# q and softmax weights read from PSUM in a gathered graph attention, with the last block as its own chunk

## The chip, the cores and the metric

The kernel runs on one core of one Trainium2 chip. The metric is the device time of one execution in microseconds; before the change it is 3077.46 us, the median of three runs (3075.20 to 3083.46). The profile is of one more execution, which took 2989.22 us, with a span of 2987.4 us from the first to the last instruction.

A core has a TensorE (PE, with its weight loads listed apart as PEld), a VectorE (DVE), a ScalarE (ACT) and a GpSimd (POOL), which run their instructions in order and wait for each other by semaphores. Transfers are carried out by 16 DMA engines. SBUF is the working memory, PSUM the memory that PE writes its products to[...].

## The reference

Four graph layers follow each other on 3327 nodes of 256 features. The adjacency matrix is sparse (each entry set with probability 0.0048, about 16 neighbours a node). Layer 0 is a simpler attention; layers 1 to 3 are transformer layers whose attention is masked by the adjacency:

```python
qkv = layer_norm(x, g1, be1) @ w_qkv
q, k, v = ...                                   # [n, 8 heads, 32]
scores = jnp.einsum('nhd,mhd->hnm', q, k) * SCALE
scores = jnp.where(mask, scores, -jnp.inf)      # mask: adj != 0
attn = jax.nn.softmax(scores, axis=-1)
out = jnp.einsum('hnm,mhd->nhd', attn, v).reshape(n, DIM)
x = x + out @ w_proj + b_proj
h2 = layer_norm(x, g2, be2)
ff = jax.nn.gelu(h2 @ w1 + b1) @ w2 + b2        # 256 -> 1024 -> 256
return x + ff
```

## The kernel before

A first part builds each node's list of neighbours, sorts the nodes by degree into 26 blocks of 128 nodes, and computes layer 0. What follows concerns the second part, layers 1 to 3. Block b has CAPS[b] neighbour slots per node (40 for block 0, then 24 down to 10). For each slot, GpSimd gathers the K and V rows (2 KB) of 128 neighbours with one indirect DMA; four slots make a group, and a ring of ten groups holds the gathered rows. Blocks are worked in the order 25, 1, 24, 2, ..., 13, 0.

```python
CAPS = [40, 24, 22, 21, 20, 20, 19, 19, 18, 18, 17, 17, 17,
        16, 16, 15, 15, 15, 14, 14, 13, 13, 12, 12, 11, 10]
GS = 4; NBUF = 10; CB = 4

def issue(self):                                   # one group of gathers
    ...
    for s in range(n):
        nc.gpsimd.indirect_dma_start(              # L1214
            out=t[:, s, :], out_offset=None, in_=kv[L],
            in_offset=bass.IndirectOffsetOnAxis(ap=t2[:, b, k:k + 1].bitcast(U32), axis=0))

def scores(self, b, s0):
    ...
    k = t[:, :n, :D]                               # K product, in place: L1232
    nc.vector.tensor_mul(k, k, t2[:, b, None, D:2 * D].to_broadcast([P, n, D]))
    nc.vector.tensor_reduce(self.sc[b][:, s0:s0 + n, :],              # L1233
                            k.rearrange("p s (h d) -> p s h d", d=HD), AX.X, ALU.add)

def softmax(self, b):                              # the max on DVE (L1244), exp on ACT (L1247)
    ...
def weights(self, b):                              # sums, reciprocal, and sc = sc / sum (L1255)
    ...
def values(self, b, s0):
    ...                                            # V product: L1269
    nc.vector.tensor_mul(vw..., v, self.sc[b][:, s0:s0 + n, :, None].to_broadcast(...))
    for s in range(0, n, 2):                       # PE adds the slots up, with an identity: L1274
        nc.tensor.matmul(self.po[b][:, :m], ident, vw[:, s * D:s * D + m], ...)
    self.issue()                                   # the group's buffer is free again
    if s0 + GS >= S:
        self.short += self.block(b)
```

When a block's values are summed, six short steps project it: copy po (ACT), transpose (PE), copy (ACT), project (PE), nothing, add to x (DVE, L1314). Four blocks make a chunk; once the last of them is projected, the chunk's long steps are queued: norm, transposes, and a feed-forward network on up to 512 columns (up L1352, gelu L1358, down L1367, all with features on partitions), a transpose back (L1373, L1381), an add (L1385), and then the next layer's norm and q, k, v (L1396), stored to DRAM for the next layer's gathers. In layer 3 the rows are scattered to the output instead (L1409). Both queues are taken from between groups:

```python
def some(self):
    for _ in range(2 if len(self.short) > 6 else 1):
        if self.short:
            self.short.pop(0)()
    self.credit = min(self.credit + self.rate, 8.0)
    while self.long and self.credit > 0:
        cost, step = self.long.pop(0)
        self.credit -= cost
        step()

def run(self):
    ...
    for k, b in enumerate(ORDER):
        ...
        for g in slots[b]:
            self.scores(*g)
            ...                                    # one or two values() of earlier blocks
            self.some()
        self.softmax(b)
        ...
    while todo:
        value()
        self.some()
    self.rate = 4.0
    while self.short or self.long:
        self.some()
```

The eight PSUM banks are 2 for po, 2 for the feed-forward sums, 1 for the projection, 3 for everything else. With 26 blocks and chunks of four, the last chunk has two blocks, 13 and 0. The next layer's first gather can start only when all rows of K and V are stored.

Of the kernel before, what the change touches and what calls it, by code (L numbers as in the profile page):

```python
# [17 lines left out]
P = 128  # L18
N = 3327
D = 256  # L20
# [503 lines left out]
def sparse_path(ctx, tc, ins, out, dram, flag):  # L524
# [614 lines left out]
    ps_y = ctx.enter_context(tc.tile_pool(name="b_ps_y", bufs=2, space=PSUM))  # L1139
    ps_r = ctx.enter_context(tc.tile_pool(name="b_ps_r", bufs=1, space=PSUM))  # L1140
    ps_b = ctx.enter_context(tc.tile_pool(name="b_ps_b", bufs=3, space=PSUM))

# [8 lines left out]

    bp3 = big.tile([96, D], BF, name="bp3")
    nc.vector.memset(bp3, 0.0)

    def bank(name):
        return ps_b.tile([P, 512], FP, tag="b", name=name)

    def load_rest(L):
        w = gains(L, ("g2", "be2", "b1", "b2"), wts, bank, "b")
        for name, c, n in (("w_proj", 2, D), ("w1", 2, FF), ("w2", 8, D)):  # L1160
            w[name] = wts.tile([P, c, n], FP, tag=name, name=f"s_{name}_{L}")
            nc.sync.dma_start(w[name], get(L, name).rearrange("(c p) n -> p c n", p=P))
        room = work.tile([P, 2 * D], FP, tag="kvr", name=f"s_row_{L}")
        row, part3 = room[:96, :D], room[:96, D:D + D // 2].bitcast(BF)
        nc.vector.memset(row, 0.0)
        for p in (0, 32, 64):
            nc.sync.dma_start(row[p:p + 1, :], get(L, "b_proj")[None, :])
        for p in (0, 32, 64):
            nc.vector.tensor_copy(part3, row)
            nc.vector.tensor_copy(bp3[p:p + 1, :], part3[p:p + 1, :])  # L1170
            if p < 64:
                nc.vector.tensor_sub(row, row, part3)
        return w
# [7 lines left out]
    ORDER = [b for k in range(NB // 2) for b in (NB - 1 - k, k + 1)][:NB - 1] + [0]  # L1181
    CHUNK = {}
    for k, b in enumerate(ORDER):
        first = k // CB * CB
        CHUNK[b] = ORDER[first:first + CB]
    slots = {b: [(b, s) for s in range(0, CAPS[b], GS)] for b in ORDER}

    class Layer:
        def __init__(self, L, w, nxt):
            self.L, self.w, self.nxt = L, w, nxt  # L1190
            self.groups = [g for b in ORDER for g in slots[b]]
            self.issued = 0
            self.tiles, self.sc, self.po = {}, {}, {}
            self.rows = 0

            self.short, self.long = [], []
            self.rate = self.credit = 0.0
# [20 lines left out]


        def scores(self, b, s0):  # L1220

            L, S = self.L, CAPS[b]
            n = min(GS, S - s0)
            t = self.tiles[b, s0]
            if s0 == 0:
                self.sc[b] = work.tile([P, LMAX, HEADS], FP, tag="sc", bufs=3, name=f"sc_{L}_{b}")
                if L == 1:
                    nc.vector.tensor_scalar(pad[b],
                                            t2[:, b, 2 * D:2 * D + S].bitcast(I32),
                                            0.0, FAR, ALU.is_equal, ALU.mult)  # L1230
            k = t[:, :n, :D]
            nc.vector.tensor_mul(k, k, t2[:, b, None, D:2 * D].to_broadcast([P, n, D]))  # L1232
            nc.vector.tensor_reduce(self.sc[b][:, s0:s0 + n, :],  # L1233
                                    k.rearrange("p s (h d) -> p s h d", d=HD), AX.X, ALU.add)
            if L == 1:
                nc.scalar.copy(t2[:, b, 2 * D + s0:2 * D + s0 + n].bitcast(I32), t[:, :n, 2 * D])
# [12 lines left out]
        def weights(self, b):  # L1249
            L, S = self.L, CAPS[b]  # L1250
            sc = self.sc[b][:, :S, :]
            den = small.tile([P, HEADS], FP, tag="den", name=f"den_{L}_{b}")
            nc.vector.tensor_reduce(den, sc.rearrange("p s h -> p h s"), AX.X, ALU.add)
            nc.vector.reciprocal(den, den)
            nc.vector.tensor_mul(sc, sc, den[:, None, :].to_broadcast([P, S, HEADS]))  # L1255
            nc.vector.tensor_max(least, least, den)

        def values(self, b, s0):
# [4 lines left out]
            if s0 == 0:  # L1263
# [6 lines left out]
                vw[:, :n * D].rearrange("p (s h d) -> p s h d", h=HEADS, d=HD), v,  # L1270
                self.sc[b][:, s0:s0 + n, :, None].to_broadcast([P, n, HEADS, HD]))
            for s in range(0, n, 2):
# [9 lines left out]
        def block(self, b):  # L1282
# [7 lines left out]
            def copy():  # L1290
                c["o"] = work.tile([P, 2 * D], FP, tag="o", name=f"o_{L}_{b}")
                nc.scalar.copy(c["o"], self.po.pop(b))  # L1292

            def turn():
                pt = c["pt"] = bank(f"pto_{L}_{b}")
                for k in range(2):
# [5 lines left out]
            def copy_T():  # L1302
                c["oT"] = work.tile([P, 2 * P], FP, tag="oT", name=f"oT_{L}_{b}")
                nc.scalar.copy(c["oT"], c["pt"][:, :2 * P])

            def project():
                ps = c["ps"] = ps_r.tile([P, 512], FP, tag="r", name=f"ppr_{L}_{b}")
                nc.tensor.matmul(ps[:, :D], ones_bf[:96, :], bp3, start=True, stop=False)
                for k in range(2):
                    nc.tensor.matmul(ps[:, :D], c["oT"][:, k * P:(k + 1) * P], w["w_proj"][:, k, :],  # L1310
                                     start=False, stop=(k == 1))

            def add():
                nc.vector.tensor_add(x, x, c["ps"][:, :D])  # L1314
                n2.stats(chunk.index(b), x)
                if b == chunk[-1]:
                    self.long += self.chunk(chunk, n2)
                    at = ORDER.index(b) + 1
                    turns = sum(len(slots[i]) for i in ORDER[at:at + CB])
                    self.rate = sum(cost for cost, _ in self.long) / max(turns - 2, 1)  # L1320

            return [copy, turn, copy_T, project, lambda: None, add]

        def chunk(self, blocks, n2):
# [10 lines left out]
            def turns(key, tag):  # L1335
                def turn(j):
                    if j == 0:
                        c[tag] = [bank(f"p{tag}_{L}_{b0}_{k}") for k in range(2)]
                    c[key].turn(j, x[j], work, c[tag])
# [21 lines left out]
            def down(f):  # L1361
                if f == 0:
                    c["py"] = [ps_y.tile([P, 512], FP, tag="y", name=f"py_{L}_{b0}_{k}")
                               for k in range(2)]
                g = c.pop(("gT", f))
                for e in range(2):
                    nc.tensor.matmul(c["py"][e][:, :n], w["w2"][:, f, e * P:(e + 1) * P],  # L1367
                                     g[:, :n], start=(f == 0), stop=(f == FF // P - 1))

# [6 lines left out]
            def back(j0):  # L1376
                pb = c["pd", j0] = bank(f"pd_{L}_{b0}_{j0}")
                for j in js[j0:j0 + 2]:
# [12 lines left out]
            def qkv(j):  # L1391
                b = blocks[j]
                pk, pq = c["pk", j], c["pq", j] = bank(f"pk_{L}_{b}"), bank(f"pq_{L}_{b}")
                for ps, c0, c1 in ((pk, D, 3 * D), (pq, 0, D)):
# [26 lines left out]
            F = FF // P  # L1421
            for f in range(F + 3):
                fs = []
                if 0 <= f - 2 < F:
                    fs.append(lambda f=f: gelu(f - 2))
                if 0 <= f - 3 < F:
                    steps.append(at(2 * k, *fs, lambda f=f: down(f - 3)))
                    fs = []
                if f < F or fs:
                    steps.append(at(2 * k, *fs, *([lambda f=f: up(f)] if f < F else [])))  # L1430
            steps += [at(1.5, shift), at(1.5, lambda: back(0))]
            if len(blocks) > 2:
# [15 lines left out]
        def some(self):  # L1448

            for _ in range(2 if len(self.short) > 6 else 1):  # L1450
                if self.short:
                    self.short.pop(0)()
            self.credit = min(self.credit + self.rate, 8.0)
            while self.long and self.credit > 0:
                cost, step = self.long.pop(0)
                self.credit -= cost
                step()

        def run(self):
            for _ in range(NBUF):  # L1460
                self.issue()

            todo, wait = [], {}
# [6 lines left out]
            for k, b in enumerate(ORDER):  # L1470
                while k > 2 and todo and todo[0][0] == ORDER[k - 3]:
                    value()
                for g in slots[b]:
                    self.scores(*g)
                    for i in wait:
                        wait[i] += 1
                    for _ in range(2 if len(todo) > NBUF // 2 else 1):
                        if todo and wait[todo[0][0]] > 1:
                            value()
                    self.some()  # L1480
                self.softmax(b)
                todo += slots[b]
# [52 lines left out]
```

## Time and profile before

| | |
|---|---|
| time, median of 3 | 3077.46 us |
| span of the profiled run | 2987.4 us, mean granted TensorE clock 0.81 |
| busy | PE 68%, DVE 65%, POOL 54%, ACT 25% |
| gathers of K and V (L1214) | 1344, 1132 ns each in the mean |
| K products (L1232), reductions (L1233), V products (L1269) | 363 of each, 416.0, 414.0 and 409.1 us |
| moved | 453.66 MB, 152 GB/s in the mean |

A group row of the profile names the line, the engine, the operation, what it writes and reads, how often, then its busy time, the mean duration of one, and the idle time of its engine before it with what ended it. POOL is busy only while it executes a gather's instruction; the transfer follows on the DMA engines. A window's row gives each engine's busy time and, in brackets, its instructions. Matmuls in fp32 appear as two records each.

### The profile page before, as it was taken

What the parts mean: (1) busy time and instruction counts of PE and PEld (TensorE: products, weight loads), DVE (VectorE), ACT (ScalarE), POOL (GpSimd) and SP (SyncE); (2) the same over time, 40 slices, a digit from 0 to 9 for tenths busy, and PEclk for the clock granted to TensorE, in tenths of its full rate; (3) what the DMA queues carried; (4) which work ended last, traced back from release to release, by engine and by line L of the source; (5) the groups of instructions that cost most, each with busy time, mean ns of one, the idle gap of its engine ahead of it and who ended that gap; (6) DMA issues with size and microseconds to landing.
All of it is one profiled execution on the core that took longest, in us unless ns stands there. A gap on an engine that the chain in (4) does not pass through costs nothing. (4 is left out here: it accounts for less than half of the span.)

```text
span 2987.4 us, 22161 instructions
## 1 busy us (share of the span) xinstructions
PE 2042.1 (68%) x6718; PEld 1113.3 (37%) x6718; DVE 1941.2 (65%) x3998; ACT 754.3 (25%) x1231; POOL 1615.1 (54%) x1461
## 2 busy tenths in 40 slices
PE   4566666514678878787267878787844668668757
PEld 4444444302334444344123444344322334323324
DVE  2977777556777777762477877687336766667652
ACT  2444344100223232232002222232210122222211
POOL 3000000047777777740777777777037777777750
PEclk9677676656898989898578989888966888889878
DMA  4323231147776776661666666666146656556650
GB/s 173 138 101 112 105 121 52 32 160 193 195 201 184 199 198 194 191 136 46 185 182 180 187 182 176 187 180 186 40 122 187 181 160 175 164 166 181 171 141 12
DMA packets 144459, 453.66 MB, mean 152 GB/s; under 512 B 29512, under 2 KB 40138, under 8 KB 141003
## 3 DMA queue, kind: packets, MB, share of 16 engines
q0 software_dynamic: 113056, 370.26, 44.9%
q1 hardware_dynamic: 9816, 53.89, 5.1%
q10 hardware_dynamic: 21458, 28.02, 2.6%
q8 instruction: 54, 0.88, 0.1%
q14 instruction: 75, 0.61, 0.1%
HBM read 420.63 MB, written 31.42 MB: 151 GB/s over the span
## 5 line engine op out<-in xcount | busy, mean ns | idle before, releaser
L1214 POOL DMA_INDIRECT kv<-kv,t x1344 | 1521.7, 1132 | 658.3 <-issue 349.7
L1274 PE MATMUL po<-vw,s_ident 128*128 128x512 f32 (+1 forms) x1380 | 751.6, 681 | 490.2 <-DVE vw L1269 490.0
L1232 DVE TENSOR_TENSOR kv<-kv,t 128x1024 f32<-128x1024 f32 (+3 forms) x363 | 416.0, 1146 | 463.6 <-DMA kv<-kv,t 444.5
L1274 PEld LDWEIGHTS po<-vw,s_ident 128*128 128x128 f32 x1380 | 286.4, 218 | 855.9 <-DVE vw L1269 538.8
L1269 DVE TENSOR_TENSOR vw<-kv,sc 128x1024 f32<-128x1024 f32 (+3 forms) x363 | 409.1, 1139 | 37.2 <-PE po L1274 36.1
L1233 DVE TENSOR_REDUCE sc<-kv 128x32 f32<-128x1024 f32 (+3 forms) x363 | 414.0, 1141 | 12.5
L1352 PE MATMUL pu<-fT,s_w 128*128 128x512 f32 (+1 forms) x672 | 301.5, 582 | 1.3 <-ACT fT L596 1.3
L1367 PE MATMUL py<-gT,s_w 128*128 128x512 f32 (+1 forms) x672 | 291.8, 563 | 0.0
L702 POOL MEMSET s_abf<- 128x1 bf16 x26 | 2.6, 103 | 436.9 <-PE s_ptb L714 251.5
L1352 PEld LDWEIGHTS pu<-fT,s_w 128*128 128x128 f32 x672 | 133.0, 202 | 129.4 <-issue 113.2
L1358 ACT ACTIVATE gT<-pu,pvb 128x512 f32<-128x512 f32 (+1 forms) x168 | 110.1, 657 | 278.1 <-PE pu L1352 277.9
L1367 PEld LDWEIGHTS py<-gT,s_w 128*128 128x128 f32 x672 | 127.7, 191 | 128.6 <-issue 123.9
L714 PE MATMUL s_ptb<-s_ident_bf,s_abf 128*128 128x128 bf16 x676 | 76.5, 292 | 114.6 <-ACT s_aT L715 83.4
L1292 ACT COPY o<-po 128x512 f32<-128x512 f32 x78 | 45.4, 582 | 361.6 <-PE po L1274 361.3
L591 PE MATMUL pf<-s_ident,xn_f 128*128 128x128 f32 x156 | 45.9, 445 | 130.5 <-ACT xn_f L588 130.5
L1314 DVE TENSOR_TENSOR t<-t,ppr 128x256 f32<-128x256 f32 x78 | 32.5, 417 | 144.5 <-PE ppr L1310 144.3
L1299 PEld LDWEIGHTS pto<-s_ident,o 128*128 128x128 f32 x624 | 103.8, 238 | 56.6 <-issue 45.6
L724 DVE MAX8 cand<-s_v 128x8 f32<-128x208 bf16 x416 | 117.5, 360 | 0.9
L1176 POOL DMA_INDIRECT t<-t,perm x26 | 29.5, 1136 | 157.4 <-DMA colsb<-in_L_gnn_be_dram 149.8
L714 PEld LDWEIGHTS <-s_abf 128*128 128x128 bf16 x676 | 65.5, 135 | 127.7 <-issue 93.7
L1299 PE MATMUL pto<-s_ident,o 128*128 128x128 f32 x624 | 102.5, 319 | 4.1 <-ACT o L1292 4.1
L1396 PE MATMUL pk<-s_w_qkv,nT 128*128 128x512 f32 x208 | 101.7, 613 | 2.4 <-ACT nT L596 2.4
(276 smaller groups left out, 2349.7 us busy)
## 6 DMA issues: line engine op xcount, KB each, us to landing
s_a<-in_adj_dram SPq DMA_DIRECT2D x25, 1663.5 KB
kv<-kv,t POOLq DMA_INDIRECT x1344, 3.8
kv<-kvr ACTq DMA_DIRECT2D x52, 256.0 KB
kv<-s_kvr ACTq DMA_DIRECT2D x26, 256.0 KB
s_w<-in_L_gnn_w_dram SPq DMA_DIRECT2D x6, 1024.0 KB
t<-ql ACTq DMA_DIRECT2D x6, 592.0 KB
t<-s_x ACTq DMA_DIRECT2D x6, 512.0 KB
s_w_qkv<-in_L_gnn_w_qkv_dram SPq DMA_DIRECT2D x3, 768.0 KB
```

Of the source, the lines that this page charges most:

```text
L714: nc.tensor.transpose(pt[:, m, :], self.abf[:, k * P:(k + 1) * P], ident_bf)
L724: nc.vector.max(out=self.cand[:, s, :], in_=v[:, s, :])
L1214: nc.gpsimd.indirect_dma_start(out=t[:, s, :], out_offset=None, in_=kv[L], in_offset=bass.IndirectOffsetOnAxis(ap=t2[:, b, k:k + 1].bitcas ...
L1232: nc.vector.tensor_mul(k, k, t2[:, b, None, D:2 * D].to_broadcast([P, n, D]))
L1233: nc.vector.tensor_reduce(self.sc[b][:, s0:s0 + n, :], k.rearrange("p s (h d) -> p s h d", d=HD), AX.X, ALU.add)
L1269: nc.vector.tensor_mul(vw[:, :n * D].rearrange("p (s h d) -> p s h d", h=HEADS, d=HD), v, self.sc[b][:, s0:s0 + n, :, None].to_broadcast([ ...
L1274: nc.tensor.matmul(self.po[b][:, :m], ident, vw[:, s * D:s * D + m], start=(s0 + s == 0), stop=(s0 + s + 2 >= S), skip_group_check=True)
L1299: nc.tensor.matmul(pt[:, k * P:(k + 1) * P], c["o"][:, k0:k0 + P], ident, start=(h == 0), stop=(h == 1))
L1352: nc.tensor.matmul(c["pu", f][:, :n], w["w1"][:, e, f * P:(f + 1) * P], c["hT"][:, e, :n], start=(e == 0), stop=(e == 1))
L1358: nc.scalar.activation(g[:, :n], c.pop(("pu", f))[:, :n], AF.Gelu_apprx_tanh, bias=w["b1"][:, f:f + 1])
L1367: nc.tensor.matmul(c["py"][e][:, :n], w["w2"][:, f, e * P:(e + 1) * P], g[:, :n], start=(f == 0), stop=(f == FF // P - 1))
L1396: nc.tensor.matmul(ps[:, :c1 - c0], c["hT"][:, e, j * P:(j + 1) * P], nxt["w_qkv"][:, e, c0:c1], start=(e == 0), stop=(e == 1))
```

## The change

Five things change together.

1. ACT copies the q of a block to PSUM (`take_q`), and the K product reads it there; the normalised softmax weights are written to PSUM too, and the V product reads them there, for every block but block 0, whose 40 x 8 weights do not fit. The two tiles take one PSUM bank each. The copy of the next q is placed right behind the exp of a block's softmax, which moves to the last group of the block.
2. To find the two banks, the projection's transposes and product go into po's own bank, and the transposes, feed-forward sums and q, k, v share the rest.
3. The chunks become 3, 4, 4, 4, 4, 4, 2, 1 blocks, so that block 0, the last, is a chunk by itself. For a chunk of one block the second feed-forward product is node-major (the gelu output is the stationary operand), its bias b2 is added by a matmul of ones, and no transpose back is needed.
4. Two projection steps are taken per group, one before and one after the long steps, and two values() per group during block 0.
5. The feed-forward steps are ordered anew: up(f) with gelu(f-1), then down(f-2).

```diff
+    q2 = ps_q.tile([P, 2, D], FP, name="q2")
+    w2 = ps_q.tile([P, 2, D], FP, name="w2")
...
+        def take_q(self, b):
+            self.q[b] = q2[:, ORDER.index(b) % 2, :]
+            nc.scalar.copy(self.q[b], t2[:, b, D:2 * D])
...
-            nc.vector.tensor_mul(k, k, t2[:, b, None, D:2 * D].to_broadcast([P, n, D]))
+            nc.vector.tensor_mul(k, k, self.q[b][:, None, :].to_broadcast([P, n, D]))
...
-            nc.vector.tensor_mul(sc, sc, den[:, None, :].to_broadcast([P, S, HEADS]))
+            wp = self.wp[b] = sc
+            if S * HEADS <= D:
+                wp = w2[:, ORDER.index(b) % 2, :S * HEADS]
+                wp = self.wp[b] = wp.rearrange("p (s h) -> p s h", h=HEADS)
+            nc.vector.tensor_mul(wp, sc, den[:, None, :].to_broadcast([P, S, HEADS]))
...
-                self.sc[b][:, s0:s0 + n, :, None].to_broadcast([P, n, HEADS, HD]))
+                self.wp[b][:, s0:s0 + n, :, None].to_broadcast([P, n, HEADS, HD]))
...
-    for k, b in enumerate(ORDER):
-        first = k // CB * CB
-        CHUNK[b] = ORDER[first:first + CB]
+    for n in [CB - 1] + [CB] * ((NB - CB - 2) // CB) + [2, 1]:
+        for b in ORDER[at:at + n]:
+            CHUNK[b] = ORDER[at:at + n]
+        at += n
...
+                if len(blocks) == 1:
+                    py = c["pd", 0] = c["py"][0]
+                    nc.tensor.matmul(py[:, :D], g[:, :P], w["w2"][:, f, :], start=(f == 0),
+                                     stop=False)
+                    if last:
+                        nc.tensor.matmul(py[:, :D], ones_bf[:96, :], bias3[:, 1, :], start=False,
+                                         stop=True)
+                    return
...
         def some(self):
-            for _ in range(2 if len(self.short) > 6 else 1):
-                if self.short:
-                    self.short.pop(0)()
+            if self.short:
+                self.short.pop(0)()
             ...
+            if self.short:
+                self.short.pop(0)()
...
                 for g in slots[b]:
                     self.scores(*g)
+                    if g == slots[b][-1]:
+                        self.softmax(b)
+                        if k + 1 < NB:
+                            self.take_q(ORDER[k + 1])
                     ...
-                    for _ in range(2 if len(todo) > NBUF // 2 else 1):
+                    for _ in range(2 if len(todo) > NBUF // 2 or b == 0 else 1):
                         if todo and wait[todo[0][0]] > 1:
                             value()
                     self.some()
-                self.softmax(b)
```

## The prediction

> **What bounds the kernel now.** I read the windows first: one from a layer's first K/V gather to its last (448 gathers), one for each stretch after it.
>
> ```profile
> core 0: us, PE busy (x) PEld busy (x) DVE busy (x) ACT busy (x) POOL busy (x), PEclk, DMA share, GB/s
> 635.00:1316.00 681.00, 488.36 (x1367) 247.99 (x1368) 484.30 (x808) 168.99 (x375) 529.17 (x471) 0.84 0.72 198
> 1316.00:1424.00 108.00, 84.65 (x246) 46.74 (x244) 33.01 (x85) 27.49 (x51) 0.11 (x1) 0.89 0.19 50
> 1424.00:2094.00 670.00, 488.18 (x1361) 248.01 (x1362) 482.36 (x782) 154.91 (x256) 512.64 (x448) 0.84 0.65 183
> 2094.00:2205.00 111.00, 86.23 (x252) 47.42 (x250) 35.26 (x92) 29.38 (x51) 0.00 (x0) 0.90 0.17 47
> 2205.00:2897.00 692.00, 464.83 (x1187) 221.68 (x1188) 459.13 (x669) 131.85 (x197) 530.39 (x468) 0.81 0.61 172
> 2897.00:2987.00 90.00, 55.64 (x167) 31.67 (x165) 25.82 (x51) 13.61 (x24) 6.09 (x6) 0.83 0.11 23
> ```
>
> The three layers fill 2352 of 2987 us; the 635 us before them the change does not touch. POOL at 76 to 78% busy looks hardly worse than PE or DVE at 66 to 73%. But in the timeline nearly every gather has 0.30 us of idle time before it that is ended by its own issue: 471 x 0.30 = 141, and 529 + 141 = 670 of the 681 us. **POOL never rests in a gather window.** The waits agree: DVE's longest is for a gather to land ("DVE kv L1232 <- DMA kv<-kv,t", 444.5 us), while POOL waits for the V product, which frees the gather buffers, 10.0 us in all. The stretches after the last gather (108, 111, 90 us: the tails) are another matter: POOL is empty and the last blocks' work drains.
>
> Then one gather: the line's answer, and a piece of the timeline.
>
> ```profile
> L1214 POOL DMA_INDIRECT kv<-kv,t x1344: 940/946/1996, 635.3 to 2895.4; - x192
> ```
> ```profile
> 1499.08 0.94 POOL L1214 DMA_INDIRECT kv<-kv,t  x1 [0.30 <-issue]
> 1499.11 2.37 DVE L1269 TENSOR_TENSOR vw<-kv,sc 128x1024 f32<-128x1024 f32 x2
> 1500.33 1.97 POOL L1214 DMA_INDIRECT kv<-kv,t  x1 [0.30 <-DVE vw L1269]
> ...
> 1504.02 1.22 DVE L1233 TENSOR_REDUCE sc<-kv 128x32 f32<-128x1024 f32 x1
> 1505.12 0.94 POOL L1214 DMA_INDIRECT kv<-kv,t  x1 [0.30 <-issue]
> 1505.15 1.22 DVE L1269 TENSOR_TENSOR vw<-kv,sc 128x1024 f32<-128x1024 f32 x1
> 1506.36 0.95 POOL L1214 DMA_INDIRECT kv<-kv,t  x1 [0.30 <-issue]
> ```
>
> Median 946 ns, but mean 1132 (the costliest groups) and a maximum of 1996. The gather at 1500.33 starts inside a V product and ends 0.82 us after it; the one at 1505.12 starts just ahead of a V product, or inside the reduction, and is not held. Sorting all 1344 gathers of the trace by what DVE was running when they started: 337 inside a K product (L1232) took 0.32 us too much on average, 220 inside a V product (L1269) 0.64 us; 216 inside the reduction (L1233), and the 37 inside the two adds that read one operand from PSUM (L1314, L1385), took 0.00. So (1132 - 946) x 1344 = **250 us of POOL's queue are gathers held by products of two SBUF operands**: 79, 89 and 83 us in the three layers.
>
> [...] Here the 128x256 add with a PSUM operand takes 417 ns and the 128x256 V product 416, so I count 0. [...]
>
> **The change, part by part.**
> (1) *q and weights in PSUM.* All 363 K products and the V products of every block but block 0 (its 40 x 8 weights don't fit 256 columns) lose their second SBUF operand. Block 0's V products run mostly after POOL's last gather, so nearly the whole 250 us can go, and 5 us more of the row gathers at L1176 ((1136 - 946) x 26). Cost: 78 copies of q on ACT, about 0.4 us each (a 128x256 copy, L1304, takes 368 ns), on an engine busy 19 to 25%.
> (2) *A new wait.* The first K product of a block now waits for ACT's copy, which stands behind the previous block's exp. From the max (L1244) to the end of its exp the 78 blocks of the trace take 1.2 us in the median, 3.3 in the mean, 9.4 at the 90th percentile (ACT stuck behind a gelu or copy that waits for PE; 40 of the 78 also reload the table, 1.28 us). Add 0.4 and take off the 1.2 to 2.4 us of V products DVE does meanwhile: 1.5 to 2.5 us a block, 26 blocks, 39 to 65 us per layer of DVE waiting.
> (3) *Can DVE follow?* Layer 1: busy 484, waits for the projection 41 (122 us of L1314's 144 lie in the three windows), new waits 39 to 65: 564 to 590 us. POOL without holds: 681 - 79 = 602 in layer 1, 670 - 89 = 581 in layer 2, 692 - 83 = 609 in layer 3 (where output scatters also stall it). So POOL stays the bound by a little, with DVE close behind, and two queues that close with few gathers buffered cost each other time. PE: 512-wide products start two per 1.72 us, at which rate the layer-1 window holds about 430 us of products in what would be 602. It follows, at a better clock if anything. I keep three quarters of the 255: **-190 us**.
> (4) *Last block its own chunk, second product node-major.* Ordering the instructions of both programs and pricing matmuls at that rate, PE has 78.7 us left after a layer's last K product (61.0 in layer 3); after the change 61.3 (40.9), because chunks of 2 and 1 close sooner. The final chunk now runs from 1384.1 to 1424.5, 40.4 us: its FFN (16.1 us of PE) halves, -7; one of two qkv products, -2.6; transposing back (1405.7 to 1407.3), -1.6; half the adds and copies, -1.5: -12.7. The remaining -7 come from chunks finished earlier. I take -20, -20 and -22 (layer 3 also saves a scatter, 3.2 us): **-62 us**.
> (5) *Two projection steps per group* shorten the chain that holds po. It matters in the tail, counted there; but project and add now lie one group apart, not two, which may lengthen the 41 us wait.
> (6) *Loading b2 as well*: three more row transfers and wider casts at a layer's start, where DVE waits 6 us for its first gather anyway: +4 us for two boundaries.
> Sum: -190 - 62 + 4 = **-248 us**.
>
> **Rivals.** *A: DVE becomes the bound.* If the q waits reach 4 us a block and the projection waits double, DVE needs 484 + 82 + 104 = 670 and the windows hardly move; only the tails stay, -60 us. For it: the 9.4 us at the 90th percentile. Against: half the exps come within 1.2 us, and softmax now stands ahead of the group's other work in ACT's queue. *B: PSUM reads cost more.* [...] The equal 416 and 417 ns speak against it, though at 256 columns only. *C: the transfers bind.* DMA share 0.72 in layer 1 would rise to about 0.81 at 602 us; landing stays at 3.8 us in the median but reaches 10.8. Worth 10 to 20 us in layer 1 at most. *D: all the held time comes back*, -255 - 62: about 2760 us.
>
> **Range and chances.** 3077.5 - 248 = 2829; the timed runs are 3% longer than the profiled one (2989.2), and if a gain scales with that it is 255: I say **2825 us**. The low end, 2745, is rival D scaled; the high end, 2920, keeps under half of the POOL gain and two thirds of the tails. Only A in full comes near 3016, the 2% line. Chances: faster by over 2% 0.91, within 0.07, slower 0.02.
>
> **What the profile after should show.** (1) The gather's mean at 950 to 970 ns, few above 1.1 us[...]. (2) K and V products still at 1.22 us[...]. (3) A new DVE wait for ACT's q, 100 to 200 us in all; above 300 it is A. (4) Windows of about 620, 600 and 625 us; "DVE <- DMA kv" well below 444 us. (5) Tails near 88, 91 and 68 us. What would make me wrong: DVE stalls on PE and ACT that show up as POOL waiting for V products (10 us now), since the ten gather buffers come free only after them.

## The result, and the profile after

The changed kernel takes **3336.27 us** (median of four runs, 3331.76 to 3341.51), the kernel before in the same comparison 3076.33 (3073.31 to 3083.46): a ratio of 1.0842, 95% interval [1.0814, 1.0869]. It is 8.4% slower; 2825 was predicted.

The runs of this study fell on five chips, and the kernel before takes 3068, 3091 and 3082 us on three of them (the first kind below) and 2989 and 2993 on two (the second kind). The 3091 is the median of five runs; two more on that chip, in a slower state, are left out. The granted TensorE clock of the kernel before is 0.800 to 0.812 on the first kind and 0.810 to 0.816 on the second. The result, with 3076 us for the kernel before, stands on a chip of the first kind. The profile of before that the prediction was read from spans 2987 us, as on the second kind. So each ratio below is to the kernel before on the same chip. Each of the five was used in one stretch of time only, so the runs do not tell a lasting trait of a chip from a passing condition.

The windows of the changed kernel, from each layer's first gather to its last and from there to the next (columns as in the prediction):

```profile
core 0: us, PE busy (x) PEld busy (x) DVE busy (x) ACT busy (x) POOL busy (x), PEclk, DMA share, GB/s
634.96:1435.13 800.17, 534.52 (x1371) 255.12 (x1371) 477.68 (x799) 169.34 (x393) 447.48 (x471) 0.81 0.59 168
1435.13:1560.39 125.26, 87.67 (x288) 53.96 (x288) 46.93 (x123) 33.86 (x71) 0.00 (x1) 0.83 0.19 52
1560.39:2329.10 768.71, 528.86 (x1371) 254.76 (x1371) 476.44 (x772) 157.57 (x279) 425.61 (x448) 0.83 0.56 158
2329.10:2454.80 125.70, 87.96 (x288) 54.01 (x288) 48.61 (x127) 34.80 (x67) 0.00 (x0) 0.83 0.17 44
2454.80:3227.40 772.60, 455.07 (x1154) 220.28 (x1155) 448.60 (x663) 123.42 (x210) 445.96 (x467) 0.78 0.54 155
```

The gather windows are 80 to 120 us longer than in the prediction's profile, but the gathers themselves shed their holds. The gather's line, and the longest waits of POOL and of DVE (us in all, times, longest):

```profile
L1226 POOL DMA_INDIRECT kv<-kv,t x1344: 943/949/1443, 635.0 to 3226.4; - x192
```
```profile
POOL kv L1226 <- DVE vw L1289: 386.9, 68, 20.1
```
```profile
DVE t L1334 <- PE po L1330: 287.2, 35, 28.1
DVE t L1334 <- remote: 223.6, 15, 18.9
...
DVE kv L1248 <- DMA kv<-kv,t: 50.4, 23, 7.2
DVE kv L1248 <- ACT q L1234: 43.0, 26, 9.1
```

DVE hardly waits for gathers any more (50 us, from 444). It waits for the projection (L1334 is the add; 677 us of idle time before it in the groups), and POOL, out of buffers, waits 387 us for V products (10 before). "Remote" stands where the releasing event belongs to no instruction that had just ended. This piece of the timeline shows what that means (start, duration, and in brackets the idle time before it and its releaser):

```profile
932.24 1.88 PE L1373 MATMUL pu<-fT,s_w 128*128 128x512 f32 x4
...
934.07 1.03 PE L1330 MATMUL po<-s_w_proj,oT 128*128 128x256 f32 x4
...
939.48 0.95 POOL L1226 DMA_INDIRECT kv<-kv,t  x1 [0.30 <-issue]
...
940.08 1.88 PE L1396 MATMUL py<-gT,s_w 128*128 128x512 f32 x4
...
942.03 0.69 ACT L1379 ACTIVATE gT<-pu,pvb 128x512 f32<-128x512 f32 x1 [11.67 <-remote]
...
943.49 0.42 DVE L1334 TENSOR_TENSOR t<-t,po 128x256 f32<-128x256 f32 x1 [15.68 <-remote]
...
948.93 0.95 POOL L1226 DMA_INDIRECT kv<-kv,t  x1 [8.50 <-issue]
```

The projection's products (L1330) are over at 935.10, and TensorE goes on to other work until 941.96. The add needs nothing else, and starts at 943.49, 8.4 us late; the gelu of the first product at 932.24 (over at 934.12) starts 7.9 us late. POOL has stopped at 940.43, as its ten buffers wait for V products that stand behind that add.

I compared, for every instruction that waits for TensorE in layers 1 to 3, its start with the recorded ends of all it waits for, by the program's semaphores (some 40 that also wait for a transfer whose landing is not on record are left out). In this profile 103 of 769 start over 1 us late, **731 us** in all, up to 22.7 us; below, "late starts" is this number. The expectations count in starts behind VectorE and ScalarE as well: 761 us here. Of the 87 that are over 2 us late, 81 have a semaphore update of TensorE on record within 0.25 us of their start, and only 5 one at the end of the product; of the 667 that start on time, 466 have one there. In 73 of the 87 TensorE had by then done later work that ended over 1 us before. A matmul's end is modelled in these records, but with later products done, the product was not what was late: its signal was. The signals do not simply wait for TensorE to pause: some 30 of the 87 starts come while it is busy, over 50 after it has been idle for more than 0.15 us. Nor are the waiting engines slow to react: of the 121 starts in which VectorE, ScalarE or GpSimd waits for another of these three, and not for TensorE, none is over 1 us late.

### The profile page after: what moved, and what is told of

Its sections match the earlier page's. It is cut to its first block, busy times and chain, and to the rows that moved or that the text cites. A ratio compares the mean times of both kernels' runs of the same rounds, so it can differ in the third digit from the quotient of the medians.

```text
span 3329.9 us, 22700 instructions
## 1 busy us (share of the span) xinstructions
PE 2138.1 (64%) x6859; PEld 1150.0 (35%) x6859; DVE 1957.7 (59%) x4063; ACT 767.3 (23%) x1335; POOL 1362.9 (41%) x1461
## 4 chain that ended last, share of the span: by engine, by line
PE 20%; DVE 14%; issue 13%; POOL 9%; another core or an unknown queue 9%; DMA 3%; ACT 2%; DVEq 0%; POOLq 0%; SPq 0%; ACTq 0%
POOL kv L1226 9%; PE po L1294 7%; DVE kv L1248 4%; PE pu L1373 4%; PE py L1396 3%; DVE vw L1289 3%; DVE sc L1249 3%; DMA kv<-kv,t 3%; PE pk L1426 2%; PE po L1330 1%; PE po L1319 1%; PE pq L1426 1%; DVE st_f L575 0%; DVE t L1334 0%
## 5 line engine op out<-in xcount | busy, mean ns | idle before, releaser
L1226 POOL DMA_INDIRECT kv<-kv,t x1344 | 1276.8, 950 | 1243.9 <-issue 532.1
L1294 PE MATMUL po<-vw,s_ident 128*128 128x512 f32 (+1 forms) x1380 | 790.8, 711 | 493.1 <-DVE vw L1289 350.3
L1248 DVE TENSOR_TENSOR kv<-kv,q 128x1024 f32<-128x1024 f32 (+3 forms) x363 | 413.0, 1138 | 137.5 <-DMA kv<-kv,t 50.4
L1334 DVE TENSOR_TENSOR t<-t,po 128x256 f32<-128x256 f32 x78 | 32.8, 420 | 677.3 <-PE po L1330 287.2
L1289 DVE TENSOR_TENSOR vw<-kv,w 128x1024 f32<-128x1024 f32 x333 | 371.8, 1128 | 76.7 <-remote 59.8
L1373 PE MATMUL pu<-fT,s_w 128*128 128x512 f32 (+3 forms) x768 | 318.2, 548 | 43.3 <-issue 21.3
L1396 PE MATMUL py<-gT,s_w 128*128 128x512 f32 (+2 forms) x672 | 285.6, 553 | 1.3 <-ACT gT L1379 1.3
L1379 ACT ACTIVATE gT<-pu,pvb 128x512 f32<-128x512 f32 (+3 forms) x192 | 115.9, 609 | 310.4 <-PE pu L1373 168.7
L1319 PE MATMUL po<-s_ident,o 128*128 128x128 f32 x624 | 101.7, 314 | 94.8 <-ACT o L1312 65.0
L1319 PEld LDWEIGHTS po<-s_ident,o 128*128 128x128 f32 x624 | 92.3, 221 | 137.4 <-ACT o L1312 88.1
L1330 PEld LDWEIGHTS po<-s_w_proj,oT 128*128 128x128 f32 x312 | 62.3, 222 | 184.3 <-issue 176.5
```

What stands on the lines that cost most here:

```text
L1226: nc.gpsimd.indirect_dma_start(out=t[:, s, :], out_offset=None, in_=kv[L], in_offset=bass.IndirectOffsetOnAxis(ap=t2[:, b, k:k + 1].bitcas ...
L1248: nc.vector.tensor_mul(k, k, self.q[b][:, None, :].to_broadcast([P, n, D]))
L1289: nc.vector.tensor_mul(vw[:, :n * D].rearrange("p (s h d) -> p s h d", h=HEADS, d=HD), v, self.wp[b][:, s0:s0 + n, :, None].to_broadcast([ ...
L1319: nc.tensor.matmul(pt[:, k * P:(k + 1) * P], c["o"][:, k0:k0 + P], ident, start=(h == 0), stop=(h == 1))
L1330: nc.tensor.matmul(ps, c["oT"][:, k * P:(k + 1) * P], w["w_proj"][:, k, :], start=False, stop=(k == 1))
L1373: nc.tensor.matmul(c["pu", f][:, :n], w["w1"][:, e, f * P:(f + 1) * P], c["hT"][:, e, :n], start=(e == 0), stop=(e == 1))
```

## The experiments

Theories at the start: **R**, the signals come late where gathers follow each other without holds; **P**, VectorE's reads of PSUM delay them; **S**, the new order of steps makes the stalls.

### First chip: which part is it, and is it the bytes?

**e1**: operands in SBUF again, the rest of the change kept.

```diff
-            self.q[b] = q2[:, ORDER.index(b) % 2, :]
-            nc.scalar.copy(self.q[b], t2[:, b, D:2 * D])
+            self.q[b] = t2[:, b, D:2 * D]
...
-            if S * HEADS <= D:
-                wp = w2[:, ORDER.index(b) % 2, :S * HEADS] ...
```

> The changed kernel with one part undone: the K products read q and the V products read the weights from SBUF again; the two PSUM tiles and the copies of q are gone, everything else of the change stays. Theory R (when the gathers follow each other every 1.25 us without holds, what waits for TensorE is released many microseconds late): the gather mean is back near 1130 ns, the late starts (761 us in the changed kernel's profile) all but vanish, the gather windows return to 670-690 us and the shorter tails stay; 2990 to 3070 us. Rival S (the new order of steps, one bank shared by sum, transpose and projection, two banks for the first FFN product): the stalls stay, and the held gathers come on top; 3330 us or more. Rival P (DVE's and ACT's PSUM traffic slows TensorE): as R, 2990 to 3070.

**e2**: a pause behind each gather.

```diff
                     in_offset=bass.IndirectOffsetOnAxis(ap=t2[:, b, k:k + 1].bitcast(U32), axis=0))
+                nc.gpsimd.memset(pace[:, :128], 0.0)
```

> The changed kernel with a 128x128 memset on GpSimd behind every one of the 1344 K/V gathers, so that the gathers come further apart; PSUM operands and everything else unchanged. A memset should cost POOL 0.15 to 0.3 us. Theory R: late starts fall from 761 us to under 200, windows from 770-800 to about 1.45 x 448 = 650 to 700 us, time 3000 to 3150: faster with more work. Rivals S and P: the memset only adds, or hides in POOL's waiting (387 us of it); 3330 to 3450 us.

**e3**: the kernel before with the operands alone moved.

```diff
+    qw = ps_q.tile([P, 2, D], FP, name="qw")        # one bank; b_ps_b has 2 buffers, not 3
...
+                nc.vector.tensor_copy(qw[:, 0, :], t2[:, b, D:2 * D])
-            nc.vector.tensor_mul(k, k, t2[:, b, None, D:2 * D].to_broadcast([P, n, D]))
+            nc.vector.tensor_mul(k, k, qw[:, 0:1, :].to_broadcast([P, n, D]))
...                                                   # weights likewise in qw[:, 1, :]
-                pt = c["pt"] = bank(f"pto_{L}_{b}")
+                pt = c["pt"] = ps_r.tile([P, 512], FP, tag="r", name=f"ppr_{L}_{b}")
-                ps = c["ps"] = ps_r.tile([P, 512], FP, tag="r", name=f"ppr_{L}_{b}")
+                ps = c["pt"][:, D:]
```

> The kernel before with the operands alone moved: q (copied by DVE) and the weights in one PSUM bank; for that bank the first FFN product has two banks instead of three and transpose and projection share the bank the projection had. Order of steps, chunks and node-major product as before. Gather mean expected 950 to 970 ns. Theory R: as slow as the changed kernel or nearly, 3200 to 3400 us, with several hundred us of late starts. Rival S: a gain, 2830 to 2950 us. Rival P: 3200 to 3400, so R and P are not told apart here, but by the paced run.

**e4**: half the bytes in layers 2 and 3; V is left out there.

```diff
-KVW = {1: 528, 2: 512, 3: 512}
+KVW = {1: 528, 2: 256, 3: 256}
...
-            v = t[:, :n, D:2 * D].rearrange(...)
+            v = t[:, :n, v0:v0 + D].rearrange(...)     # v0 = D in layer 1, else 0
```

> The changed kernel with rows of 256 instead of 512 floats in the K/V tables of layers 2 and 3 (V is left out, the V product uses the K half, so the result is another); layer 1 unchanged[...]. Theory R in the form 'the transfers in flight hold up the release': late starts and windows of layers 2 and 3 fall, from 769 and 773 to 600-650 us, layer 1 stays at 800; 3000 to 3100 us. [...] Rivals S and P: all three windows stay, within 2% of 3336.

Measured, beside 3067.76 us for the kernel before: e1 3123.9 (1.0178 [1.011, 1.0247]), late starts 181 us; e2 3271.17 (1.067 [1.0594, 1.0746]), 610 us; e3 3327.54 (1.0842 [1.077, 1.0915]), 813 us; e4 3345.18 (1.091 [1.0828, 1.0992]), 737 us, windows of layers 2 and 3 at 787 and 769. In the old order the moved operands, with the one bank taken for them, make the whole loss (e3). In the new order taking them back brings the ratio from 1.084 to 1.018 (e1); R expected the whole loss back (3070 us at most), but 181 us of late starts remain. S falls as the main cause. Bytes don't matter here: layers 2 and 3 move 78 and 80 GB/s instead of 156 and 154, and their windows are no shorter. So R falls in the form that puts the delay down to the transfers in flight; that the stream of gathers brings it, whatever its bytes, stays open. The memset (221 ns) brought the ratio from 1.084 to 1.067 only, far less than R expected (under 3150 us), though S and P expected no gain at all.

### Second chip: no late signals at all

**f0** is the kernel before again; **f2** keeps only q in PSUM (the weights as in e1).

> The kernel before, unchanged, profiled a second time. Its first profile spans 2987 us with no late start behind TensorE, while its timed runs take 3048 to 3089. If late starts come in every kernel now and then, this profile has up to 100 us of them; if the kernel before is free of them, it has none, and a span near 2990 again.

> The changed kernel with only q in PSUM: the V products read their weights from SBUF again and hold gathers (141 us of the 250), the K products don't. Theory R (missing holds: a gather stream without gaps delays TensorE's signals) and theory P (reads of PSUM by VectorE delay them) both put it between 3124 (all operands in SBUF) and 3336: R about 3220, late starts 400 to 550 us, as a bit over half of the holds remain; P about 3230, since half of the PSUM reads remain. It gives the size for the next two runs.

**f3** moves the holds to another instruction, and leaves the true scores out:

```diff
-            nc.vector.tensor_reduce(self.sc[b][:, s0:s0 + n, :],
-                                    k.rearrange("p s (h d) -> p s h d", d=HD), AX.X, ALU.add)
+            nc.vector.tensor_mul(k, k, k)
+            nc.vector.tensor_copy(self.sc[b][:, s0:s0 + n, :],
+                                  k.rearrange("p s (h d) -> p s h d", d=HD)[:, :, :, 0])
```

> The changed kernel with PSUM operands as they are, but the reduction over the K product replaced by a product of the same tile with itself (two SBUF operands, 128x1024, as long as the reduction) and a small copy of 1 column per head into the scores: the holds come back at another instruction, the PSUM reads stay; the scores are not the reference's. Theory R: gather mean 1.05 or more, late starts fall from 761 to under 400, 3100 to 3230 us although DVE has 448 small copies more. Theory P: the late starts stay at 700 and over, 3340 to 3450 us.

**f4** is e1 without the K product:

```diff
-            nc.vector.tensor_mul(k, k, self.q[b][:, None, :].to_broadcast([P, n, D]))
+            nc.vector.tensor_reduce(self.sc[b][:, s0:s0 + n, :],
+                                    k.rearrange("p s (h d) -> p s h d", d=HD), AX.X, ALU.add)
```

> All operands in SBUF as in e1, but each K product is replaced by a second reduction of the same tile (one SBUF operand, the same duration), so q is left out of the scores: the K holds go and no PSUM operand comes. To be compared with the run that has q alone in PSUM. Theory R: as slow as that run, 3200 to 3250, late starts as there. Theory P: as fast as all operands in SBUF or faster, 3000 to 3124, late starts at or under 217.

Of f0's two cases the second came: no late starts, and a span near 2990. The other three expectations were written for the first chip and missed: the kernel before takes 2988.82 here, f0 2993.17, f2 2958.22 (0.9898 [0.9865, 0.9931]), f3 2986.16 (0.9991 [0.9972, 1.0011]), f4 2959.42 (0.9897 [0.9865, 0.993]). None has a start more than 1.4 us late behind TensorE. That gave theory **C**: late signals come on some chips and not on others. The pair also shows something else: f2 and f4 agree within 1.2 us, so taking away the K holds is worth the same with a PSUM operand (and its copies of q) as without one; the PSUM read itself costs nothing that shows in the time.

### Third chip: the changed kernel is a gain there

g0 is the kernel before, g1 the changed kernel, g2 is e1 again and g3 is f3 again.

> The kernel before, once more. It took 3068 us on the chip of the first four runs and 2989 on that of the second four, whose profile had no late start behind TensorE. Theory C: the late signals are a trait of some chips, and the kernel before has some too there. On a chip where its timed runs take about 3070, this profile shows 60 to 120 us of late starts and a span near 3070; on one where they take about 2990, none and 2990. Against C: no late starts at 3070, so the 80 us are something else.

> The changed kernel, unchanged, on a chip of either kind. Theory C: where the kernel before takes about 2990, there are no late starts, and the change is a gain: windows of 620 to 660 us, 2830 to 2930 us. Where the kernel before takes about 3070 it is near 3336 again. Against C: 3300 or more beside a kernel before at 2990.

> The changed kernel with all K/V operands in SBUF, once more. Theory C: beside a kernel before at 2990 it has no late starts; what is left is the rest of the change alone, which the prediction puts at 60 us of gain (2930), though the run with q alone in PSUM suggests less, as its stretches after the last gather stayed at 111 us: 2960 to 3000 expected. Beside a kernel before at 3070: 3124 as in the first run.

> PSUM operands kept, holds put back at the reduction, once more. Beside a kernel before at 2990: 2986 again. Beside one at 3070 it tells R from P: R (late signals come where gathers are not held) 3080 to 3200 us and late starts under 400; P (they come from PSUM reads) 3340 to 3450, late starts 700 and over.

The kernel before takes 2993.0 (g0 2983.26), and the **changed kernel 2907.45: 0.9704 [0.9677, 0.9732], 3% faster**; of its 769 starts behind TensorE none is late. g2 takes 3014.1 (1.0065 [1.0041, 1.0089]), g3 2986.8 (0.9985 [0.9971, 0.9998]). C holds: the same program is 3% faster on one chip and 8.4% slower on another. Its windows of layers 1 and 3 here, and DVE's waits in layer 1:

```profile
634.00:1308.00 674.00, 506.96 (x1387) 248.02 (x1388) 481.12 (x801) 172.33 (x399) 445.75 (x471) 0.87 0.70 200
1308.00:1423.60 115.60, 82.71 (x274) 50.80 (x271) 43.67 (x119) 31.52 (x65) 0.00 (x0) 0.82 0.20 56
...
2212.00:2822.00 610.00, 450.77 (x1216) 212.98 (x1217) 459.68 (x673) 129.08 (x219) 444.70 (x467) 0.88 0.68 195
```
```profile
DVE t L1334 <- PE po L1330: 109.7, 16, 11.3
DVE kv L1248 <- ACT q L1234: 24.5, 16, 4.9
DVE kv L1248 <- DMA kv<-kv,t: 17.6, 12, 3.3
```

The same of the kernel before (g0):

```profile
633.00:1318.00 685.00, 492.95 (x1369) 250.70 (x1370) 484.90 (x808) 169.24 (x375) 530.02 (x471) 0.84 0.71 197
...
2199.00:2891.50 692.50, 463.08 (x1187) 221.93 (x1188) 458.52 (x669) 131.93 (x197) 530.41 (x468) 0.82 0.61 172
```
```profile
DVE kv L1232 <- DMA kv<-kv,t: 125.8, 57, 5.0
DVE t L1314 <- PE ppr L1310: 48.8, 14, 7.6
```

and with all operands in SBUF (g2), where L1329 is the add:

```profile
DVE t L1329 <- PE po L1325: 113.6, 16, 11.2
```

Layer 3 gets its gain (692 to 610 us). In layers 1 and 2 (674 and 672; before 685 and 667) the wait for the projection takes most of it: 110 and 113 us, where the kernel before has 49 and 62. In g2 it is 114 and 130 already, so the rest of the change brings it, not the operands.

### Fourth chip: R against P

h1 puts the add one step later; h2 is e3 again; h3 is the kernel before with f4's edit (q left out of the scores); h4 is e3 with f3's edit.

```diff
-            return [copy, turn, copy_T, project, lambda: None, add]
+            return [copy, turn, copy_T, project, lambda: None, lambda: None, add]
```

> The changed kernel with one more empty step between projection and add, so that about two groups of work lie between them as in the kernel before, and two steps per group still. Beside a kernel before at 2990: theory W (the wait for the projection, 110 and 113 us in the windows of layers 1 and 2 where the kernel before has 49 and 62, took their gain) expects those waits back near 50 and 60, the two windows at 610 to 640 and 2800 to 2850 us. Rival V (VectorE and TensorE have no more room there, the wait only moves): waits for the V products or for TensorE elsewhere instead, 2880 to 2910. Beside a kernel before at 3070: 3250 to 3340, late starts as in the changed kernel, since nothing of their cause is touched.

> The kernel before with q and weights in PSUM and nothing else of the change, once more. Beside a kernel before at 2990 it is the operands' gain alone in the old order: theory W 2790 to 2850 (the prediction's 190 us, or a little less), rival V 2880 to 2910, as little as the 107 us that the operands bring in the new order (3014 to 2907). Beside one at 3070: 3327 again.

> The kernel before with each K product replaced by a second reduction of the same tile (one SBUF operand, same duration; q is left out of the scores): the K holds go (about 110 us of the 250), no PSUM operand comes. Beside a kernel before at 2990: 2900 to 2940, since in the new order the same step brought 55 us (3014 to 2959). Beside one at 3070: theory R (late signals where gathers are not held) 3150 to 3250 and 300 us of late starts or more; theory P (they come from PSUM reads) 2980 to 3070, late starts under 100.

> The kernel before with q and weights in PSUM as in e3, but its reductions replaced by a product of the tile with itself (two SBUF operands, same duration) and a small copy: holds at another instruction. Beside a kernel before at 2990: 2900 to 2990. Beside one at 3070: theory R 3070 to 3200 and late starts under 400 us; theory P 3330 to 3450 and late starts of 800 us or more, as with the operands alone (868 us).

The kernel before takes 3091.22 here, a chip of the first kind. h1 takes 3381.17 (1.0974 [1.0881, 1.1068]), h2 3331.7 (1.0792 [1.0684, 1.09]), **h3 3224.97 (1.0429 [1.0331, 1.0527])**, h4 3259.97 (1.0553 [1.0469, 1.0636]). In h3 no K or V product reads PSUM; it only lacks the K holds, and has 741 us of late starts, as R expected (300 or more). Its longest waits of DVE:

```profile
DVE t L1315 <- PE ppr L1311: 192.9, 29, 21.5
DVE vw L1270 <- remote: 171.2, 28, 13.5
```

P falls: PSUM reads aren't needed for late signals. h4, with half of the holds back, lies between the two expectations (755 us late) and by itself decides nothing. The later add (h1) is no gain here.

### Fifth chip: slower gathers, a faster kernel

k1 is h1 again. **k2** is e2 with a memset twice as wide:

```diff
+                nc.gpsimd.memset(pace[:, :256], 0.0)
```

> The changed kernel with one more empty step between projection and add, once more. Beside a kernel before at 2990: theory W 2800 to 2850 us, with waits for the projection back near 50 and 60 us in layers 1 and 2; rival V (the wait only moves) 2880 to 2910. Beside one at 3070 to 3100: 3381 again.

> The changed kernel with a 128x256 memset on GpSimd behind every K/V gather: gathers some 1.63 us apart where the kernel before has 1.52 in the mean, none held. Beside a kernel before at 2990: POOL is the bound, 448 x 1.63 = 730 us a window, 2990 to 3080. Beside one at 3070 to 3100: if gaps are what counts, late starts under 200 us, windows near 730, 3130 to 3200 (the changed kernel: 3336, with a 128x128 memset 3271); if only holds help, late starts of 500 us and more and 3250 to 3350.

The kernel before takes 3081.94, so this is the first kind again. k1 takes 3369.64 (1.0931 [1.0858, 1.1004]), and **k2 3038.2: 0.9854 [0.9793, 0.9916]**. With 1344 memsets of 329 ns more, and nothing else, the changed kernel goes, on chips of this kind, from 8.4% slower than the kernel before to 1.5% faster. That is faster than its own expectation (3130 to 3200), and its late starts are 56 us (under 200 expected). A memset as such is not the cure: e2 has one behind each gather, too, and 610 us of late starts. The groups of POOL's gather and memset (busy, mean ns, idle before), the waits that stood at 387 and 50 us above, and the window of layer 1:

```profile
L1227 POOL DMA_INDIRECT kv<-kv,t x1344 | 1278.5, 951 | 547.2 <-issue 253.9
...
L1230 POOL MEMSET pace<- 128x256 f32 x1344 | 441.6, 329 | 0.7
```
```profile
POOL kv L1227 <- DVE vw L1291: 54.5, 39, 5.0
```
```profile
DVE kv L1250 <- DMA kv<-kv,t: 262.4, 113, 7.5
```
```profile
635.14:1363.20 728.06, 521.82 (x1400) 251.53 (x1401) 492.04 (x806) 173.47 (x401) 593.17 (x919) 0.85 0.67 185
```

POOL hardly waits for V products, DVE waits for gathers again, and the windows are 728, 693 and 692 us instead of 800, 769 and 773. Nobody holds these gathers (951 ns), so holds were only one way to space them. What goes with the late starts is the mean step from gather to gather within a running stream (of all steps under 2.6 us):

| kernel, chips of the first kind | step, us | late starts, us |
|---|---|---|
| e4, half bytes | 1.28 | 737 |
| changed kernel | 1.29 | 731 |
| h1 and k1, later add | 1.27 | 911 and 906 |
| e3, operands alone | 1.29 | 813 |
| h2, e3 again | 1.29 | 883 |
| h4, PSUM and holds | 1.36 | 755 |
| e2, memset of 128 | 1.36 | 610 |
| h3, no K holds | 1.37 | 741 |
| e1, SBUF operands | 1.43 | 181 |
| k2, memset of 256 | 1.44 | 56 |

It is a mean: in e1 and h3 about as many steps are the shortest ones, of 1.25 us (881 and 875), and what differs is how much holds add to the others (236 and 120 us of time over 945 ns). A limit for a single step is not shown.

On the second kind 1.29 us (g1) and 1.37 us (f2) go with no late start, and so does the kernel before with 1.45. The kernel before was never profiled on the first kind; why it takes 75 to 100 us more there, and whether it has late starts at its step of 1.45 us, was not seen.

k2 beats both kernels on the first kind of chip. On the second it was not run; its windows of 692 us would make it about as fast as the kernel before there, which is an estimate, so the changed kernel stays the fastest run on those.

## Why the prediction was wrong

**The miss of the result** was not in a term of the sum but in what the sum left out. Step (3), "POOL without holds: 681 - 79 = 602 in layer 1" and so on, failed: it took the released gathers as free of side effects. On the result's chip the windows became 800, 769 and 773 us instead. With a gather every 1.29 us, where the prediction's profile has 1.45, TensorE's signals came up to 23 us late, 731 us in all, and the prediction's own warning came true, DVE stalls on PE and ACT that show up as POOL waiting for V products: 387 us. No view of the profile before could show it, since by its time it came from a chip of the second kind, where no step that was run does this.

**(1) Holds.** Right on both kinds: 950 and 947 ns in the mean, no more holds (6.7 and 3.8 us over 945 ns). *The -190 us* was too large even where nothing is late: from g2 to g1 the operands bring 3014 to 2907, 107 us. Layer 3 gave 80 of its 83; layers 1 and 2 gave 20 each of 79 and 89. Here "waits for the projection 41" in step (3) was mis-sized: with the new order it was 114 and 130 us with no operand moved (step (5) had said that project and add one group apart may lengthen this wait, but gave it no cost). So DVE (481 us busy, 110, 25 and 18 of waits) is taken for 634 of the 674 us, and shorter waits fill most of the rest. Rival A was right in layers 1 and 2, by the projection and not by q. The test on a chip without late signals, the later add, fell twice on the other kind, where it is no gain (1.097 and 1.093); so that the wait can be had back is not shown. In all, the second kind gives -107 + 21 = -86 us where the sum said -248; the 21 stand under (4), (5).

**(2) K and V products, rival B.** Right: 1218 and 1215 ns in the mean for 128x1024 with a PSUM operand, 1226 and 1219 before.

**(3) The wait for q.** 100 to 200 us expected, 43 us measured on the result's chip and 50 in g1's windows: mis-sized, two to four times too large.

**(4), (5) Tails.** 88, 91 and 68 us expected; 125, 126 and 103 in the result, and 116, 116 and 81 in g1, against 104, 110 and 90 in g0. With SBUF operands (g2) they are 108, 107 and 80. PE's busy time there did fall, from 82, 86 and 56 us (g0) to 76, 74 and 49 (g2), but its idle time rose from 22 to 32 us in layer 1. I priced the queue of PE's work. By g1's timeline, though no run tests it, the tail ends with a chain of hand-offs, and three chunks of 4, 2 and 1 blocks have one chain each (in g1, 2.6 us of thirteen small norm operations on DVE, then ACT, then PE, before each chunk's products). So -62 + 4 became +21 us for the whole rest of the change (g2 against the kernel before). How it splits between chunks, order and the loading of b2 was not tried.

**Rival C, transfers bind.** Half the bytes gained nothing on the first kind, so bandwidth is not what binds there; on the second kind this was not tried.

**Range and chances.** They rested on one profile of one chip. The timed runs were 3% longer than that profile, and I scaled the gain by it; by the runs above it is the mark of another kind of chip. The low end is also off by its own rule: rival D scaled by 3% is 2751, not 2745.

## What to carry to other kernels

An engine that runs ahead can do harm: before freeing a stream of indirect gathers, try it paced as well, since on the first kind of chip 329 ns of idle work behind each gather was worth some 300 us (from 8.4% slower to 1.5% faster). When a profile and its timed runs differ by 3%, find out why first. Compare starts with what each instruction waits for: when all its producers are done by the records, and later work on their engine too, look at the signal: in the changed kernel's profile 81 of the 87 latest starts have an update of TensorE on record within 0.25 us of them.

## What the runs showed of the hardware

- On three of five chips, and where the result was taken, TensorE's semaphore updates come up to 20 us and more late (22.7 in the changed kernel) when 128-row indirect gathers follow each other closely: with a mean step of 1.37 us (h3) 741 us of delay in the whole run, with 1.43 us (e1) 181 and with 1.44 us (k2) 56. On two chips no start is over 1.4 us late, in eight profiles with steps of 1.29 to 1.46 us. Signals of VectorE and ScalarE are not delayed so (in the changed kernel none of 121 starts).
- The delay ends when the stream does or in the middle of it: of the 87 longest, 33 end with gathers still running, the others after POOL's last one, mostly 2.5 to 4.8 us after.
- Rows of 1 KB instead of 2 KB don't change it: 737 us of late starts in e4, 731 in the changed kernel. The profile of before holds 22752 semaphore updates by its 1422 indirect transfers, 16 each. In the changed kernel's profile on the first kind only 9167 of them are on record, in g1's all. But records of other updates are missing there too (1041 of 1248 of TensorE's, 2556 of 3171 of VectorE's), and k2, with hardly a late start, has 17385 of the 22752; so gaps in the record do not measure the delay. Whether TensorE's signals wait for these updates was not shown, nor what differs between the chips.
- A 128x128 fp32 memset on GpSimd took 221 ns (e2), a 128x256 one 329 ns (k2), and part of it went into the 0.30 us that lies before each gather anyway: the commonest step grew from 1.25 to 1.33 and 1.44 us.
